# An edge loop of a graph network: fewer chunks by one-hot products, with source and target rows taken the same way

## The chip, the core and the metric

The kernel runs on one core of one Trainium2 chip. TensorE (PE) multiplies matrices into PSUM, VectorE (DVE) and ScalarE (ACT) do elementwise work, GpSimd (POOL) here issues the indirect transfers, and SyncE (SP) issues plain ones. Each engine works through its own queue in order and waits on semaphores. The metric is the device time of one execution in microseconds. The kernel before took 853.11 us, the median of three runs (850.22 to 855.66).

## The reference, cut to what matters

The whole network has four graph layers and four feed-forward layers on 384 nodes of 512 features. The change touches the first graph layer only, and of it only the scores of the 6144 edges. It has 8 heads (H0), and each head works on 128 numbers (2 x HD0) of a row of 1024 (EW):

```python
p = x @ Ww[:512]                 # source part, one row of 1024 for each node
q = x @ Ww[512:] + bw            # target part
s = p[src] + q[dst]              # one row for each edge
score[edge, head] = sum(leaky_relu(s[head's 128 columns], 0.01) * Wa) + ba
```

The kernel writes leaky_relu as 0.01 of the number itself plus 0.99 of its positive part. The first part is linear, so it is worked out once for each node: 8 numbers for a source (`plin`) and 8 for a target, which are columns 1024 to 1031 of the target's row (EL is 1032). Only the positive part has to be worked out for each edge.

## The kernel before, in words

**Set-up.** x is normalized and turned (`xT`). Four weight tiles give first q, then p, in three tiles of 128 nodes and two halves of 512 columns each (`project`, f32). A q tile gets its bias on DVE (L394), its linear part by `linear` (L360, L362), and is stored to `qd` in DRAM from SP. A p tile is copied from PSUM by ACT and stored to `pd`. It is also kept in SBUF as three bf16 parts (`split`): the number rounded to bf16, the rest rounded to bf16, and what then is left (ACT L408 and L412, DVE L411 and L413). The sum of the three parts holds the f32 number nearly whole.

**Edge loop.** The edges go in 48 chunks (EC) of 128, one edge for each partition. There are two ways to a chunk's rows. A *transfer chunk* fetches p's rows into `gp` and q's rows into `gq` by indirect DMAs from POOL (L430, L436), FETCH = 7 chunks ahead, adds them on DVE (L507), and takes the positive part times 0.99 Wa (L509). A *product chunk* fetches only `gq`. Its source rows come from PE: the one-hot matrix `os` of the chunk's sources is turned by three transposes (L384), copied to SBUF by ACT (`osT`, L386), and multiplied with the three tiles and three parts of p (nine bf16 products for each half, L461). The target rows are added in the same PSUM sum by one f32 product with the identity (L463), and DVE reads the sum from PSUM (L516). `by_products` sends 21 chunks this way and 27 by transfers.

For every chunk DVE makes the one-hots `os` and `od` (L371, L372) and copies the target's 8 linear numbers to `lin8` (L503). PE counts edges into `pc` by three products of `os` and `od` (L465). ACT sums seven of the eight heads (L520, an activation and a read of its accumulator for each), and DVE sums the eighth and adds the linear part (L476, L477). POOL then scatters the 8 numbers of each edge into a table in DRAM (`mats`, L446), LAG = 2 chunks later.

**Order.** In one turn c of the loop the code issues: fetches for chunk c+7, scatter of c-2, one-hots of c+3, their turning for c+2, products of c+1, and then chunk c's own work on DVE and ACT. The `issue_after` blocks hold the groups in this order, but between them instructions may be moved, so ACT's copies of turned one-hots stand somewhere between the sums of two chunks. Buffers also hold the order: three PSUM banks `mm` for the sums of products, two `tp` for transposes, five `gp`, eight `gq`, and six `w8` for the 8 numbers, which come free when their scatter has landed. After the loop the table is read back, and the rest of the network follows.

Of the kernel before, what the change touches and what calls it, by code (L numbers as in the profile page):

```python
# [8 lines left out]
F32 = mybir.dt.float32  # L9
F16 = mybir.dt.float16  # L10
BF16 = mybir.dt.bfloat16
# [25 lines left out]
AHEAD = 4  # L37
GQ_BUFS = 8
FETCH = 7
LAG = 2  # L40
# [53 lines left out]
def gnn_ffn_kernel(ctx: ExitStack, tc: tile.TileContext, a, out: bass.AP):  # L94
# [225 lines left out]
    with ExitStack() as s1:  # L320
# [37 lines left out]
        def linear(dst, sb):  # L358
            lin = spare_n[:, 0:2, :].rearrange("p a d -> p (a d)")
            V.tensor_mul(lin.rearrange("p (h k) -> p h k", h=H0),  # L360
                         sb[:, :EW].rearrange("p (h k) -> p h k", h=H0), bc(wa_lin, heads, 1))
            return V.tensor_reduce(dst, lin.rearrange("p (h k) -> p h k", h=H0), AX.X, OP.add)  # L362
# [4 lines left out]
        def hots(c):  # L367

            os_ = ep.tile([P, N], BF16, name="os")
            od = ep.tile([P, N], BF16, name="od")  # L370
            V.tensor_scalar(os_, nodes16, srcf[:, c:c + 1], None, op0=OP.is_equal)  # L371
            V.tensor_scalar(od, nodes16, dstf[:, c:c + 1], None, op0=OP.is_equal)  # L372
            hot[c] = os_, od

        def by_products(c):
            return c < 4 or c % 5 in (1, 3)

        osTs = {}

        def hots_turned(c):  # L380
            if by_products(c):
                pT = pt.tile([P, NT, P], BF16, name="tp")
                for t in range(NT):
                    T.transpose(pT[:, t, :], hot[c][0][:, t * P:(t + 1) * P], identb)  # L384
                osTs[c] = ep.tile([P, NT, P], BF16, name="osT", bufs=2)
                S.copy(osTs[c], pT)  # L386

        ww = stream.take(4, ahead=False)
        for t in range(NT):
            sb = ep.tile([P, EL], F32, name="gq", bufs=GQ_BUFS)  # L390
            for cs in halves:
                p = ps.tile([P, D], F32, name="mm")
                shown = project(p, xT, t, lambda k: ww[k // 2][:, k % 2, cs])
                V.tensor_add(sb[:, cs], p, bw[:, cs])  # L394
            linear(sb[:, EW:], sb)
            ended = V.tensor_scalar(sb[:, EW:], sb[:, EW:], ba, None, op0=OP.add)
            nc.sync.dma_start(qd[t * P:(t + 1) * P, :], sb)

        split, srcs = [], []
        for t in range(NT):  # L400
            with tc.issue_after(shown.ins), tc.issue_after(ended.ins):
                sb = ep.tile([P, EW], F32, name="gp", bufs=5)
                pp = slot()[:, :3 * D].bitcast(BF16).rearrange(
                    "p (i n) -> p i n", i=3)
                for h, cs in enumerate(halves):
                    p = ps.tile([P, D], F32, name="mm")
                    shown = project(p, xT, t, lambda k: ww[2 + k // 2][:, k % 2, cs])
                    S.copy(pp[:, 0, cs], p)  # L408
                    S.copy(sb[:, cs], p)
                    rest = spare_t.rearrange("p k n -> p (k n)")[:, h * D:(h + 1) * D]  # L410
                    V.tensor_sub(rest, sb[:, cs], pp[:, 0, cs])  # L411
                    S.copy(pp[:, 1, cs], rest)  # L412
                    ended = V.tensor_sub(pp[:, 2, cs], rest, pp[:, 1, cs])  # L413
                nc.sync.dma_start(pd[t * P:(t + 1) * P, :], sb)
# [8 lines left out]
        with tc.tile_pool(name="pa", bufs=1, space=bass.MemoryType.PSUM) as pa:  # L423
# [9 lines left out]

            def fetch_target(c):
                gq = ep.tile([P, EL], F32, name="gq", bufs=GQ_BUFS)
                G.indirect_dma_start(out=gq, out_offset=None, in_=qd,  # L436
                                     in_offset=bass.IndirectOffsetOnAxis(ap=dsti[:, c:c + 1], axis=0))
                return gq
# [11 lines left out]
            def multiplied(c):  # L450
# [4 lines left out]
                if by_products(c):  # L455
                    gq, osT = fetched[c][1], osTs.pop(c)
                    z = [ps.tile([P, D], F32, name="mm") for h in range(2)]
                    for h, cs in enumerate(halves):
                        for t in range(NT):
                            for i in range(3):  # L460
                                T.matmul(z[h], lhsT=osT[:, t, :], rhs=split[t][:, i, cs], start=t == 0 and i == 0,  # L461
                                         stop=False)
                        T.matmul(z[h], lhsT=ident, rhs=gq[:, cs], start=False, stop=True)  # L463
                for t in range(NT):
# [13 lines left out]

            multi = {0: multiplied(0)}
            with tc.issue_after(ended.ins):  # L480
                ended = linear(plin[:, 2, :], srcs[2])
            marks = [ended]
            for c in range(EC):
# [7 lines left out]
                if c >= LAG:  # L491
                    marks.append(scatter(c - LAG))
                if c + 3 < EC:
                    hots(c + 3)
                if c + 2 < EC:
                    hots_turned(c + 2)
                if c + 1 < EC:
# [4 lines left out]
                lin = ep.tile([P, H0], F32, name="lin8")  # L502
                V.tensor_copy(lin, gq[:, EW:])  # L503
                w8 = sums[c] = ep.tile([P, H0], F32, name="w8", bufs=6)
# [1243 lines left out]
```

## Time and profile before

| | |
|---|---|
| median of three runs | 853.11 us |
| profiled execution | 855.45 us |
| its span, first to last instruction | 853.5 us |
| mean granted clock of PE | 0.93 |
| PE, DVE, ACT, POOL busy | 87%, 54%, 32%, 27% of the span |
| set-up: first projection to last split of p | 9.9 to 57.0 us |
| chunks 0 to 3, all by products | 53.6 to 79.6 us |
| chunks 4 to 47 | 79.6 to 231.3 us |
| last scatter issued | 234.9 us |

Shares over the whole span say little of the loop, since the rest of the network is a different program. The profile is therefore read by windows: the busy time of each engine between two moments. A timeline row gives start, duration, engine, line, operation, what is written and read, and in brackets how long the engine had been idle and what ended that. Rows of one engine may overlap[...]. What one instruction costs in a row of equal ones is the difference of their starts.

### The profile page before, as it was taken

The page shows a single profiled execution, that of the slowest core. Times are in us where ns is not written, and L with a number is a line of the kernel's source. Part 1 is how long each engine was busy: PE and PEld are TensorE (multiplying, and loading weights), DVE is VectorE, ACT ScalarE, POOL GpSimd, SP SyncE. Part 2 cuts the span into 40 slices and gives each one's busy share as a digit, 9 for nine tenths or more (in the row PEclk, how much of TensorE's full clock was granted, in tenths as well). Part 3 has the DMA queues.
Part 4 walks back from the last instruction along what each step waited for, and adds up shares of the span by engine and source line. Part 5 has one row for each costly group of instructions (what it writes and reads, how often), then busy time and mean ns, then how long its engine had stood idle before and what let it go on. Part 6 is the DMA issues. An engine that isn't in the chain of part 4 may idle for free.

```text
span 853.5 us, 9894 instructions
## 1 busy us (share of the span) xinstructions
PE 746.5 (87%) x2865; PEld 350.2 (41%) x2865; DVE 462.1 (54%) x1199; ACT 273.1 (32%) x1042; POOL 234.5 (27%) x230
## 2 busy tenths in 40 slices
PE   5999888898946769948789999799999999999975
PEld 3444433343434535423355544454444344333432
DVE  4575988887779665376522254745434242421227
ACT  1144766666638723333131111221111111011100
POOL 0046777777600210000100000023333233322122
PEclk9999999899968678985989999889999999999998
DMA  9987877877388011210531463298999999999982
GB/s 336 410 312 243 284 273 258 285 216 238 106 330 311 1 37 53 96 50 12 226 138 49 154 215 108 90 390 320 408 408 403 400 387 396 385 389 391 379 338 104
DMA packets 71197, 211.84 MB, mean 248 GB/s; under 512 B 11615, under 2 KB 16351, under 8 KB 70368
## 3 DMA queue, kind: packets, MB, share of 16 engines
q1 hardware_dynamic: 40592, 135.56, 41.7%
q0 software_dynamic: 19728, 57.97, 19.8%
q10 hardware_dynamic: 10816, 17.61, 5.9%
q8 instruction: 25, 0.41, 0.2%
q14 instruction: 36, 0.29, 0.1%
HBM read 188.46 MB, written 29.83 MB: 256 GB/s over the span
## 4 chain that ended last, share of the span: by engine, by line
PE 56%; DVE 20%; DMA 14%; ACT 6%; issue 3%; DVEq 0%; POOL 0%; SPq 0%; ACTq 0%; POOLq 0%
PE mm L88 14%; DMA w<-in_L_ffn_w_dram 11%; PE acc L88 9%; PE mm L290 8%; PE mm L461 6%; PE mm L1080 4%; PE acc L1093 3%; PE tp L88 3%; PE mm L463 2%; PE mm L952 2%; DVE gp L507 2%; PE acc L965 2%; ACT junk L520 2%; DVE gp L509 2%; DVE mx L88 2%
## 5 line engine op out<-in xcount | busy, mean ns | idle before, releaser
L88 PE MATMUL mm<-w,xe 128*64 128x512 f32 (+1 forms) x504 | 146.1, 598 | 4.9 <-DMA w<-in_L_ffn_w_dram 4.9
L461 PE MATMUL mm<-w,osT 128*128 128x512 bf16 x378 | 92.2, 391 | 9.9 <-ACT osT L386 9.8
L88 POOL DMA_INDIRECT xg<-xnd,src x38 | 39.3, 1034 | 164.9 <-DVE ye L88 140.8
L88 ACT ACTIVATE hide<-mm 128x256 f32<-128x256 f32 x38 | 14.6, 385 | 214.1 <-PE mm L88 214.1
L88 POOL DMA_INDIRECT parts<-ye,dst x35 | 37.9, 1083 | 154.9 <-DVE ye L88 154.9
L88 PEld LDWEIGHTS mm<-w,xe 128*64 128x64 f32 (+1 forms) x504 | 48.2, 148 | 75.0 <-issue 69.1
L88 PE MATMUL acc<-w,hT 128*64 128x512 f32 (+1 forms) x244 | 77.4, 610 | 0.0
L88 DVE TENSOR_TENSOR hide<-hide,mm 128x256 f32<-128x256 f32 x38 | 16.1, 424 | 109.0 <-ACT hide L88 109.0
L290 PE MATMUL mm<-w,xT 128*128 128x512 f32 x144 | 68.6, 633 | 1.8 <-DMA w<-in_L_gnn_Ww_dram 1.2
L520 ACT ACTIVATE junk<-gp 128x128 f32<-128x128 f32 x186 | 54.8, 296 | 39.8 <-issue 22.9
L436 POOL DMA_INDIRECT gq<-qd,dsti x48 | 50.6, 1054 | 59.8 <-DMA qd<-gq 41.8
L461 PEld LDWEIGHTS <-osT 128*128 128x128 bf16 x378 | 36.7, 100 | 65.8 <-issue 17.1
L446 POOL DMA_INDIRECT mat<-w,kidx x48 | 57.0, 1187 | 22.5 <-DMA mat<-w,kidx 4.4
L88 DVE TENSOR_SCALAR ye<-acc,wts 128x512 f32<-128x512 f32 x35 | 26.3, 750 | 59.4 <-PE acc L88 59.4
L520 ACT ACTIVATE junk<-relu 128x128 f32<-128x128 f32 x147 | 43.4, 297 | 18.3 <-DVE relu L516 10.6
L290 PEld LDWEIGHTS mm<-w,xT 128*128 128x128 f32 x144 | 28.8, 204 | 37.7 <-issue 34.4
L516 DVE SCALAR_TENSOR_TENSOR relu<-mm,wa_relu 128x512 f32<-128x512 f32 x42 | 28.1, 684 | 29.3 <-PE mm L463 29.3
L463 PE MATMUL mm<-gq,ident 128*128 128x512 f32 x84 | 43.2, 596 | 0.0
L88 PEld LDWEIGHTS tp<-ident,xg 128*128 128x128 f32 x164 | 23.6, 202 | 28.5 <-issue 24.5
L465 PE MATMUL pc<-od,os 128*128 128x384 bf16 x144 | 29.3, 330 | 6.3 <-DVE od L372 6.3
L520 ACT ACTIVATION_READ_ACCUMULATOR junk<-gp 128x1 f32 x186 | 34.8, 187 | 0.0
L509 DVE SCALAR_TENSOR_TENSOR gp<-gp,wa_relu 128x1024 f32<-128x1024 f32 x27 | 33.1, 1228 | 0.9
(370 smaller groups left out, 1210.0 us busy)
## 6 DMA issues: line engine op xcount, KB each, us to landing
w<-in_L_ffn_w_dram SPq DMA_DIRECT2D x204, 512.0 KB, 12.0
mat<-y ACTq DMA_DIRECT2D x2, 4608.0 KB, 28.4
m<-mat SPq DMA_DIRECT2D x12, 768.0 KB, 7.1
parts<-xg POOLq DMA_DIRECT2D x1, 6144.0 KB, 19.9
w<-parts SPq DMA_DIRECT2D x6, 1024.0 KB, 11.6
w<-in_L_gnn_Ww_dram SPq DMA_DIRECT2D x4, 1024.0 KB, 10.1
w<-in_L_gnn_W_dram ACTq DMA_DIRECT2D x2, 1024.0 KB, 9.0
qd<-gq SPq DMA_DIRECT2D x3, 516.0 KB, 6.7
```

The costliest lines, as they stand in the source:

```text
L88: self.last = getattr(self.engine, name)(*args, **kwargs)
L290: last = T.matmul(p, lhsT=xT[:, k, t * P:(t + 1) * P], rhs=w(k), start=start and k == 0, stop=stop and k == kc - 1)
L436: G.indirect_dma_start(out=gq, out_offset=None, in_=qd, in_offset=bass.IndirectOffsetOnAxis(ap=dsti[:, c:c + 1], axis=0))
L446: return G.indirect_dma_start(out=mats[c % 2], out_offset=bass.IndirectOffsetOnAxis(ap=kidx[:, c:c + 1], axis=0), in_=sums.pop(c), in_offs ...
L461: T.matmul(z[h], lhsT=osT[:, t, :], rhs=split[t][:, i, cs], start=t == 0 and i == 0, stop=False)
L463: T.matmul(z[h], lhsT=ident, rhs=gq[:, cs], start=False, stop=True)
L465: counts.append(T.matmul(pc[t], lhsT=os_[:, t * P:(t + 1) * P], rhs=od, start=c == 0, stop=c == EC - 1))
L509: done = V.scalar_tensor_tensor(g3, g3, 0.0, wide, op0=OP.max, op1=OP.mult)
L516: done = V.scalar_tensor_tensor(g3[:, c8, :], z[h].rearrange("p (h k) -> p h k", h=HH), 0.0, wide[:, c8, :], op0=OP.max, op1=OP.mult)
L520: summed = S.activation(j, g3[:, h, :], AF.Identity, accum_out=w8[:, h:h + 1])
L1080: T.matmul(p, lhsT=gate[:, k, c], rhs=xT[:, k, :], start=k == 0, stop=k == KC - 1)
L1093: T.matmul(p, lhsT=hid[:, m, t * P:(t + 1) * P], rhs=w2[:, m, :], start=m == 0, stop=m == 1)
```

## The change

Fifteen chunks (chunk 0 and those with c % 7 of 1 or 4) now take both source and target rows by products, and 33 take both by transfers. For this, q is also kept in three bf16 parts: its 1024 columns in two idle activation tiles and one new tile (`split_q`), its 8 linear columns in small tiles (`lin_q`). A product chunk turns both one-hots (`osT`, `odT`), sums nine products with p's parts and nine with q's in each half, and gets the 8 linear numbers by nine products of 8 columns into a third PSUM tile, taken from the two `tp` buffers. The f32 product with the identity and the target fetch of these chunks are gone. FETCH is 6, `gq` has five buffers, one-hots have five buffers and are made for chunk c+4, and turned for c+3. The scratch of `linear` is now a buffer of the `relu` ring.

```diff
-GQ_BUFS = 8
-FETCH = 7
+GQ_BUFS = 5
+FETCH = 6
...
-            lin = spare_n[:, 0:2, :].rearrange("p a d -> p (a d)")
+            lin = ep.tile([P, EW], F32, name="relu", bufs=2)
...
-            os_ = ep.tile([P, N], BF16, name="os")
-            od = ep.tile([P, N], BF16, name="od")
+            os_ = ep.tile([P, N], BF16, name="os", bufs=5)
+            od = ep.tile([P, N], BF16, name="od", bufs=5)
...
         def by_products(c):
-            return c < 4 or c % 5 in (1, 3)
+            return c == 0 or c % 7 in (1, 4)
...
             if by_products(c):
-                pT = pt.tile([P, NT, P], BF16, name="tp")
-                for t in range(NT):
-                    T.transpose(pT[:, t, :], hot[c][0][:, t * P:(t + 1) * P], identb)
-                osTs[c] = ep.tile([P, NT, P], BF16, name="osT", bufs=2)
-                S.copy(osTs[c], pT)
+                turned_hots[c] = []
+                for i, name in enumerate(("osT", "odT")):
+                    pT = pt.tile([P, NT, P], BF16, name="tp")
+                    for t in range(NT):
+                        T.transpose(pT[:, t, :], hot[c][i][:, t * P:(t + 1) * P], identb)
+                    turned_hots[c].append(ep.tile([P, NT, P], BF16, name=name, bufs=2))
+                    S.copy(turned_hots[c][i], pT)
+
+        def three(dst, part, c, src, rest):
+            S.copy(dst[:, 0, c], part)
+            V.tensor_sub(rest, src, dst[:, 0, c])
+            S.copy(dst[:, 1, c], rest)
+            return V.tensor_sub(dst[:, 2, c], rest, dst[:, 1, c])
...
+        kept = [slot() for t in range(NT)]
+        kept_q = [v.rearrange("p k n -> p (k n)") for v in (spare_t, spare_n)] + [one.tile([P, 3 * D], F32, name="qq")]
...
             nc.sync.dma_start(qd[t * P:(t + 1) * P, :], sb)
+            qq = bf16s(kept_q[t])
+            for h, cs in enumerate(halves):
+                three(qq, sb[:, cs], cs, sb[:, cs], kept[t][:, 3 * D:])
+            ql = one.tile([P, 3, H0], BF16, name=f"ql{t}")
+            ended = three(ql, sb[:, EW:], slice(0, H0), sb[:, EW:], one.tile([P, H0], F32, name="qrest"))
+            split_q.append(qq)
+            lin_q.append(ql)
...
             def fetch_target(c):
+                if by_products(c):
+                    return None
...
                     z = [ps.tile([P, D], F32, name="mm") for h in range(2)]
+                    z.append(pt.tile([P, H0], F32, name="tp"))
+                    parts_ = [(i, t) for i in range(3) for t in range(NT)]
                     for h, cs in enumerate(halves):
-                        for t in range(NT):
-                            for i in range(3):
-                                T.matmul(z[h], lhsT=osT[:, t, :], rhs=split[t][:, i, cs], start=t == 0 and i == 0,
-                                         stop=False)
-                        T.matmul(z[h], lhsT=ident, rhs=gq[:, cs], start=False, stop=True)
+                        for n, (w, whole) in enumerate(((osT, split), (odT, split_q))):
+                            for i, t in parts_:
+                                T.matmul(z[h], lhsT=w[:, t, :], rhs=whole[t][:, i, cs],
+                                         start=n == 0 and (i, t) == (0, 0), stop=n == 1 and (i, t) == (2, NT - 1))
+                    for i, t in parts_:
+                        T.matmul(z[2], lhsT=odT[:, t, :], rhs=lin_q[t][:, i, :], start=(i, t) == (0, 0),
+                                 stop=(i, t) == (2, NT - 1))
...
+            hots_turned(2)
+            hots(3)
...
+                if c + 4 < EC:
+                    hots(c + 4)
                 if c + 3 < EC:
-                    hots(c + 3)
-                if c + 2 < EC:
-                    hots_turned(c + 2)
+                    hots_turned(c + 3)
...
-                V.tensor_copy(lin, gq[:, EW:])
+                V.tensor_copy(lin, gq[:, EW:] if z is None else z[2])
```

More of the change, by code (lines that the diff above doesn't have):

```diff
@@ L375, in by_products @@
         def by_products(c):
-            return c < 4 or c % 5 in (1, 3)
-        osTs = {}
+            return c == 0 or c % 7 in (1, 4)
+        turned_hots = {}
         def hots_turned(c):
             if by_products(c):
-                pT = pt.tile([P, NT, P], BF16, name="tp")
-                for t in range(NT):
-                    T.transpose(pT[:, t, :], hot[c][0][:, t * P:(t + 1) * P], identb)
-                osTs[c] = ep.tile([P, NT, P], BF16, name="osT", bufs=2)
-                S.copy(osTs[c], pT)
+                turned_hots[c] = []
[10 more added lines that the diff above has]
+            return V.tensor_sub(dst[:, 2, c], rest, dst[:, 1, c])
         ww = stream.take(4, ahead=False)
+        kept = [slot() for t in range(NT)]
+        kept_q = [v.rearrange("p k n -> p (k n)") for v in (spare_t, spare_n)] + [one.tile([P, 3 * D], F32, name="qq")]
+        bf16s = lambda w: w[:, :3 * D].bitcast(BF16).rearrange("p (i n) -> p i n", i=3)
+        split_q, lin_q = [], []
         for t in range(NT):
@@ L395, in gnn_ffn_kernel @@
             linear(sb[:, EW:], sb)
-            ended = V.tensor_scalar(sb[:, EW:], sb[:, EW:], ba, None, op0=OP.add)
+            V.tensor_scalar(sb[:, EW:], sb[:, EW:], ba, None, op0=OP.add)
             nc.sync.dma_start(qd[t * P:(t + 1) * P, :], sb)
+            qq = bf16s(kept_q[t])
[5 more added lines that the diff above has]
+            lin_q.append(ql)
         split, srcs = [], []
@@ L402, in gnn_ffn_kernel @@
                 sb = ep.tile([P, EW], F32, name="gp", bufs=5)
-                pp = slot()[:, :3 * D].bitcast(BF16).rearrange(
-                    "p (i n) -> p i n", i=3)
+                pp = bf16s(kept[t])
                 for h, cs in enumerate(halves):
@@ L407, in gnn_ffn_kernel @@
                     shown = project(p, xT, t, lambda k: ww[2 + k // 2][:, k % 2, cs])
-                    S.copy(pp[:, 0, cs], p)
                     S.copy(sb[:, cs], p)
[L410 to L413, printed above, removed]
+                    ended = three(pp, p, cs, sb[:, cs], kept[t][:, 3 * D:])
                 nc.sync.dma_start(pd[t * P:(t + 1) * P, :], sb)
@@ L455, in multiplied @@
                 if by_products(c):
-                    gq, osT = fetched[c][1], osTs.pop(c)
+                    osT, odT = turned_hots.pop(c)
                     z = [ps.tile([P, D], F32, name="mm") for h in range(2)]
+                    z.append(pt.tile([P, H0], F32, name="tp"))
+                    parts_ = [(i, t) for i in range(3) for t in range(NT)]
                     for h, cs in enumerate(halves):
-                        for t in range(NT):
-                            for i in range(3):
-                                T.matmul(z[h], lhsT=osT[:, t, :], rhs=split[t][:, i, cs], start=t == 0 and i == 0,
-                                         stop=False)
-                        T.matmul(z[h], lhsT=ident, rhs=gq[:, cs], start=False, stop=True)
+                        for n, (w, whole) in enumerate(((osT, split), (odT, split_q))):
[5 more added lines that the diff above has]
+                                 stop=(i, t) == (2, NT - 1))
                 for t in range(NT):
```

## The prediction

> **What bounds the kernel now.** The profile's second part shows the edge loop as the stretch where POOL reads 7 (slices 4 to 11, 64 to 235 us). Only this loop and the set-up before it are changed, so I read the windows of the loop, then its waits, then the chain of waits. Columns of the first fence: PE, PEld, DVE, ACT and POOL busy us (instructions), granted clock, DMA share, GB/s.
>
> ```profile
> 79.60:231.30 151.70, 133.02 (x563) 60.69 (x562) 126.28 (x303) 100.53 (x631) 114.45 (x102) 0.97 0.73 236
> ```
> ```profile
> DVE relu L516 <- PE mm L463: 18.5, 13, 2.6
> ...
> ACT junk L520 <- DMA mat<-w,kidx: 12.9, 6, 4.4
> ...
> PE mm L461 <- ACT osT L386: 9.8, 9, 3.0
> ```
>
> At 79.6 us DVE starts chunk 4; at 231.3 it is done with chunk 47. No engine is full; three are close. POOL looks 75% busy, but its timeline shows 0.30 us of nothing ahead of every instruction, so 102 instructions cost 114.45 + 102 x 0.30 = 145.1 of 151.7 us, 1.42 us each. DVE's only real idle time is 18.5 us before the relu of a product chunk, waiting for PE. PE in turn waits for ACT's copy of the turned one-hots, and ACT now and then for a scatter that POOL sent late (its w8 ring has six buffers). The chain of waits repeats one turn per five chunks:
>
> ```profile
> 95.84 1.14 DVE gp L507
> 97.01 1.22 DVE gp L509
> 99.43 1.02 DVE gp L507
> 100.75 1.23 issue
> 101.99 2.15 ACT junk L520 x14
> 104.56 2.12 PE mm L461 x9
> 106.68 0.86 PE mm L463 x2
> 107.53 1.94 PE mm L461 x9
> 109.48 0.87 PE mm L463 x2
> 110.37 0.69 DVE relu L516
> ```
>
> Two transfer chunks on DVE, ACT's sums, then a product chunk's 5.8 us on PE in the open. From relu to relu (94.15 to 110.37) 16.2 us pass for five chunks; DVE's own work for them is 14.8 (below). The rest is the second of two product chunks that stand only two apart: its products can't start before ACT has copied the turned one-hots, which stand in ACT's queue behind the sums of two chunks.
>
> **Prices.** DVE, from its timeline: start to start a transfer chunk takes 3.39 to 3.68 us (82.46 to 86.05; 88.26 to 91.65), I take 3.45; a product chunk without a wait 2.21 to 2.32 (86.05 to 88.26), I take 2.25. PE:
>
> ```profile
> 59.67 0.33 PE L384 MATMUL tp<-identb,os 128*128 128x128 bf16 x3
> 59.84 2.11 PE L461 MATMUL mm<-w,osT 128*128 128x512 bf16 x9
> 61.78 1.02 PE L463 MATMUL mm<-gq,ident 128*128 128x512 f32 x2
> 62.64 2.10 PE L461 MATMUL mm<-w,osT 128*128 128x512 bf16 x9
> ```
>
> Start to start: nine bf16 products 1.94 us (216 ns each), one f32 product (two records) 0.86, three transposes 0.17 (55 ns each), and three counts `pc` 0.49.
>
> **The change in the loop, by engine.**
> PE: a product chunk had 18 x 0.216 + 2 x 0.86 = 5.6 us; now 36 x 0.216 = 7.8, plus nine products of 8 columns and three more transposes. No 8-column product is in the trace; each has weights of its own, as the transposes do, so I take their 55 ns: 0.5 us a chunk. The ends are 25 ns, the issue floor in the Trainium skill ("TensorE: Matmul & The Clock Gate", Back-to-back issue gap), and 81 ns, which the same section gives for pairs of weight load and 128-column matmul. That rule speaks against swapping one f32 product for strings of small ones: 15 x 9 + 45 more transposes make 180 pairs, 14.6 us by the rule, 9.9 by the row; I take the row, as this kernel's pairs ran at it. With two sets of transposes (0.33) a product chunk is 8.6 us. All chunks: 21 x 5.8 + 48 x 0.49 = 145 before, 15 x 8.6 + 23.5 = 153 after.
> DVE: six chunks go from 2.25 to 3.45: +7.2 us. The 8-wide copy from PSUM instead of from `gq` is below 0.1 either way.
> POOL: 15 target gathers go, 6 source gathers come: 123 instructions become 114, -9 x 1.42 = -12.8 us.
> ACT: 30 copies of turned one-hots instead of 21, +9 x 0.46 = 4.1 us; ACT has 51 us free in the window, and only the copies' place in the queue counts.
> DMA: 9 gathers of about 0.5 MB less, at a share of 0.73; nothing waits on a gather (L507 has no idle time before it), so nothing for that.
> Fewer buffers: with FETCH 6 and five `gp` and `gq` buffers, the gather for chunk c+6 takes the buffer of chunk c-1, so POOL can't begin turn c before DVE's reduce of c-1 is done; behind that gather on POOL stand the target gather and the scatter of c-2. The gather lands 5.8 us after issue (median of the DMA view) and is wanted six chunks, 19 us, later: no cost while POOL lags DVE by less than 13 us. `linear`'s scratch in the relu ring and q's parts in idle activation tiles move no instruction.
>
> **What decides is the order.** Product chunks now lie 3 and 4 apart, and one-hots and their turning are issued one chunk earlier. In the changed queues ACT's copies for the next product chunk stand within or just before the sums of the last one. New is a ring: z[2] and both turned one-hots share the two `tp` buffers, so the target transposes of the next product chunk wait for DVE's `lin` copy of the last; behind them on PE stand the counts and the next z, on which DVE waits.
> Gap of three, from `lin` to `lin`: DVE needs 2 transfer chunks and its own relus, 3 x 1.0 + 2 x 2.4 + 1.3 = 9.1 us. PE: transposes, counts and ACT's copy about 1.0, then 7.8 + 0.5, 0.2 to hand over: 9.5. Stall 0.4 us. Gap of four: DVE 12.5, PE 3.2 (behind seven sums, 2.05, and two copies) + 8.3 = 11.5: none. So seven chunks take about 22.0 us, 3.14 a chunk, where five took 16.2, or 3.25.
> POOL: seven chunks hold 10 gathers and 7 scatters, 17 x 1.42 = 24.1 us, more than 22.0, as before 13 x 1.42 = 18.5 against 16.2. POOL falls behind up to the w8 ring, then holds ACT, and catches up in the last chunks, which have no gathers left.
>
> **The set-up.** Its head on DVE grows: 12 subtractions at 0.61 us start to start and 6 of 8 columns, 8 us, and DVE's queue has them after the last q tile, ahead of p's splits. ACT gets 12 copies at 0.5. The p evacuations on ACT stand behind q's, but PSUM has three buffers and the first must be free at 43 us; it is at about 42. DVE from 36.1: 8 for q's splits, some 0.5 of waits on ACT, then p's 12 subtractions (7.3), three `linear` (7.3, the last behind the splits), four pairs of one-hots (1.8). The last split lands at about 59 instead of 57; PE's last projection waits for the one-hots of chunk 1 queued ahead of it and ends at 55 instead of 53.5. Then only two product chunks come, not four: z of chunk 0 ends at 63, of chunk 1 at 72 (7.8 + 0.5 + 0.5 each), and DVE starts chunk 2 at about 73.5; with 1 us for hand-overs, 74.5. The source gathers wait for the store of p (62.2 now, about 63.5 then) and the first is there by 70. So 46 chunks remain at 74.5, where 44 remained at 79.6: minus 5.1 us, but two chunks more.
>
> **The sum.** By the chain: 74.5 + 46 x 3.14 = 219; by POOL: 104 instructions remain when scatter 0 goes out at 74, 74 + 104 x 1.42 = 222 for the last scatter, which comes 4.5 us after DVE's end (235.9 against 231.3 now). Both ask for 218 to 219. The same sums for the kernel as it is give 79.6 + 44 x 3.25 = 223, and it took 231.3: 8 us went to two late scatters (4.4 and 4.1 us) and the cold clock after them. I keep half of that, since POOL still falls behind: 219 + 4 to 5 = 223.5, 7.6 us less. The profiled execution took 855.45 (span 853.5 and 1.95 around it); it would take 847.9. It lies above the median, and 853.11 - 7.6 gives **845.5**.
>
> Cold clock: after more than 2.5 us without work PE ran at half speed:
>
> ```profile
> 166.84 4.05 PE L461 MATMUL mm<-w,osT 128*128 128x512 bf16 x9
> ...
> 171.87 2.11 PE L461 MATMUL mm<-w,osT 128*128 128x512 bf16 x9
> ```
>
> This cost 1.9 us here (idle 2.5 us before) and 1.7 at 202.08 (idle 3.0). The skill's page named above (Part 1) wants an idle window of some 3.4 us; the row has it after less, and I go by the row. Changed, PE works 20.6 of 22 us, so by either no such gap should come up and up to 3.6 us come back (half taken); if gaps do, a z of 36 products starts with a run at half speed.
>
> **Rivals.**
> 1. *Full cover* (15%): with 9 POOL instructions less, no scatter is late; the loop ends at 219, total 841. For it: POOL's balance is 6% better by chunk. Against: 24.1 is still above 22.0.
> 2. *No gain* (10%): product chunks keep the stall of now, 18.5 / 17 = 1.1 us; 13 x 1.1 = 14 us on DVE's own 74.5 + 33 x 3.45 + 13 x 2.25 = 217.6 gives 232: 854. For it: PE's z is longer by 2.7 us. Against: copies are issued one chunk earlier.
> 3. *PE becomes the bound* (20%, slower): the `tp` ring chains DVE's `lin`, PE's transposes, ACT's copy and z in series. If ACT's copy falls behind the seven sums (2.05 us) and PE waits until its clock halves (1.9), each of the seven gap-of-three chunks costs 4 us: +28, total 873. From 1.1 us at each of them the gain is gone, from 2.3 on it is slower by over 1%. For it: z is 8.3 us against 9.1 of cover; any slip shows. Against: the changed order of ACT.
>
> **Numbers.** My own case (55%) reaches from 840 to 850, a little under half beyond 1% (8.5 us, what a measurement here can tell from no change). Faster 0.25 + 0.15 = 0.40; same 0.30 + 0.10 = 0.40; slower 0.20. The unknown prices (8-column products, 11 us between their ends on PE, two thirds hidden; set-up 3 us; POOL 1.42 to 1.50, 8 us) make 836 to 850 and rival 2 and the near part of 3 take it up to 858.
>
> **What would show it.** Right: DVE adds chunk 2 at 72 to 76 us; idle before the relus under 8 us in all; last scatter at 225 to 230; granted clock in the loop 0.97 or more. Wrong: PE idle on ACT's odT for over 2 us per product chunk, the last split later than 62 us, or gathers late at L507's successor.

## The result and the profile after

The changed kernel takes 855.92 us (median of 20 runs, 852.38 to 861.54); the kernel before, run beside it, 852.09 us (20 runs). The ratio is **1.0053, with a 95% interval of 1.0034 to 1.0072**: some 4.5 us slower, where 7.6 us faster was forecast. The profiled execution took 856.2 us, its span 854.1. The rest of the network is not what made it slower: from the first maximum on the table `m` to the end of the span, 609.8 us pass before and 605.8 after (602.0 to 609.8 in the 20 profiles of this document). The loss lies ahead of that point, which came at 243.69 us and now comes at 248.24. In this profile it lies behind the loop: DVE's last sum ends at 230.6 us (231.2 before), and from there to the maximum 17.7 us pass instead of 12.5. So two things need a cause: why the loop gained 0.6 us and not 7.6, and why its tail grew.

First the window of the loop in the profile after, with the columns of the prediction's first fence.

```profile
79.60:231.30 151.70, 134.57 (x775) 65.08 (x773) 133.84 (x305) 105.46 (x653) 116.07 (x99) 0.99 0.71 223
```

The clock is now 0.99 (0.97 before). PE does a little more, and DVE 7.6 us more, near the 7.2 that were forecast. The line to stop at is POOL's: three instructions less than before in the same time, and 1.6 us more busy. Then the waits in the same window, as total, number and longest in us:

```profile
ACT junk L543 <- DMA mat<-w,kidx: 18.5, 11, 4.4
...
DVE gp L530 <- DMA gp<-pd,srci: 5.7, 5, 2.1
...
DVE relu L539 <- PE mm L480: 2.8, 4, 1.3
```

DVE's wait for products fell from 18.5 us to 2.8, as forecast. Two others grew: ScalarE waits longer for landed scatters (12.9 us before), and DVE now waits for gathered rows, which it never did before. Both come from POOL. Its groups from 73 to 240 us (instructions, busy us, mean ns, idle before), first before, then after:

```profile
L446 POOL DMA_INDIRECT mat<-w,kidx x47 | 56.0, 1191 | 22.2 <-DMA mat<-w,kidx 4.4 <-DVE lin L503 3.6 <-issue 3.3
L436 POOL DMA_INDIRECT gq<-qd,dsti x38 | 40.5, 1066 | 15.3 <-issue 6.7 <-PE mm L463 4.0 <-DVE od L372 1.2
L430 POOL DMA_INDIRECT gp<-pd,srci x22 | 22.9, 1041 | 7.0 <-ACT junk L520 4.3 <-issue 1.5 <-DVE w L476 0.6
```
```profile
L463 POOL DMA_INDIRECT mat<-w,kidx x48 | 53.5, 1115 | 32.9 <-issue 17.8 <-DVE w L498 8.8 <-DVE lin L526 2.7
L453 POOL DMA_INDIRECT gq<-qd,dsti x28 | 37.1, 1325 | 8.8 <-DVE od L372 3.4 <-issue 3.4 <-DVE gp L532 0.6
L445 POOL DMA_INDIRECT gp<-pd,srci x28 | 33.2, 1186 | 8.5 <-ACT junk L543 5.5 <-issue 1.8 <-DMA mat<-w,kidx 0.9
```

Before, 107 instructions take 119.4 us, 1.12 each. After, 104 take 123.8 us, 1.19 each: a target gather costs 0.26 us more than it did. The timeline shows where from (start, duration):

```profile
132.43 1.21 DVE L530 TENSOR_TENSOR gp<-gp,gq 128x1024 f32<-128x1024 f32 x1
132.46 2.02 POOL L453 DMA_INDIRECT gq<-qd,dsti  x1 [0.30 <-DVE od L372]
```

A gather whose issue usually takes 0.94 to 0.99 us takes 2.02 when it begins just after DVE's add of `gp` and `gq` has begun. Which of the two begins first is what counts:

```profile
151.03 0.99 POOL L463 DMA_INDIRECT mat<-w,kidx  x1 [0.30 <-DVE w L497]
151.72 1.22 DVE L530 TENSOR_TENSOR gp<-gp,gq 128x1024 f32<-128x1024 f32 x1
152.33 1.45 POOL L445 DMA_INDIRECT gp<-pd,srci  x1 [0.30 <-ACT junk L543]
```

In this profile 40 issues overlap an add from 73 to 240 us. The 28 that began 0.02 to 1.06 us after it all ended 0.81 to 0.87 us after the add did, wherever inside it they began. The 12 that began before it, or together with it, took at most 1.05 us.

Below, **hold-up** is the sum, over POOL's instructions from 40 to 242 us that take more than 1.1 us, of their time above 0.96. It was 16.1 us in 23 instructions before and is 25.7 us in 33 after; 19.3 us of that lie under the add (each issue is put to the operation that it overlaps longest), nearly all the rest under DVE's other operations with two f32 operands in SBUF (3.0 us under the multiply with `wa_relu`, 2.5 under the product in `linear` in the set-up), none under the relu that reads PSUM.

The chain of waits shows what it does. Three turns of the loop go through a gather issued too late, and the end through late scatters (start, duration):

```profile
137.32 8.78 DMA gp<-pd,srci
...
163.86 8.64 DMA gp<-pd,srci
...
187.73 5.29 DMA gp<-pd,srci
```
```profile
230.39 5.09 DMA mat<-w,kidx
...
235.55 3.08 issue
...
238.84 2.63 DMA mat<-w,kidx
```

### The profile page after: what moved, and what is told of

It reads as the page before. It is cut to its first block, busy times and chain, and to the rows that moved or that the text cites. A ratio compares the mean times of both kernels' runs of the same rounds, so it can differ in the third digit from the quotient of the medians.

```text
span 854.1 us, 10391 instructions
## 1 busy us (share of the span) xinstructions
PE 745.2 (87%) x3105; PEld 354.9 (42%) x3105; DVE 478.5 (56%) x1217; ACT 282.6 (33%) x1069; POOL 235.5 (28%) x221
## 4 chain that ended last, share of the span: by engine, by line
PE 44%; DMA 27%; DVE 20%; ACT 5%; issue 3%; POOL 1%; SPq 0%; DVEq 0%; ACTq 0%; POOLq 0%
DMA w<-in_L_ffn_w_dram 20%; PE mm L88 8%; PE acc L88 7%; PE mm L480 7%; PE mm L290 6%; PE mm L1103 4%; PE acc L1116 3%; DMA gp<-pd,srci 3%; PE mm L975 2%; DVE gp L530 2%; DVE gp L532 2%; PE acc L988 2%; PE tp L88 2%; DMA m<-mat 2%; DMA mat<-w,kidx 1%
## 5 line engine op out<-in xcount | busy, mean ns | idle before, releaser
L543 ACT ACTIVATE junk<-gp 128x128 f32<-128x128 f32 x228 | 67.2, 296 | 37.3 <-issue 13.7
L88 DVE TENSOR_TENSOR hide<-hide,mm 128x256 f32<-128x256 f32 x38 | 16.1, 424 | 108.9 <-ACT hide L88 108.9
L480 PE MATMUL mm<-w,osT 128*128 128x512 bf16 x270 | 65.0, 387 | 7.7 <-ACT osT L388 7.7
L453 POOL DMA_INDIRECT gq<-qd,dsti x33 | 43.7, 1324 | 50.2 <-DMA qd<-gq 40.1
L445 POOL DMA_INDIRECT gp<-pd,srci x33 | 39.0, 1182 | 18.3 <-DMA pd<-gp 8.5
L530 DVE TENSOR_TENSOR gp<-gp,gq 128x1024 f32<-128x1024 f32 x33 | 40.2, 1219 | 5.7 <-DMA gp<-pd,srci 5.7
L480 PEld LDWEIGHTS <-osT 128*128 128x128 bf16 x270 | 26.1, 99 | 41.7 <-ACT osT L388 11.0
L543 ACT ACTIVATION_READ_ACCUMULATOR junk<-gp 128x1 f32 x228 | 42.6, 187 | 0.0
L532 DVE SCALAR_TENSOR_TENSOR gp<-gp,wa_relu 128x1024 f32<-128x1024 f32 x33 | 40.5, 1226 | 1.1
L480 PEld LDWEIGHTS <-odT 128*128 128x128 bf16 x270 | 26.4, 98 | 32.1 <-ACT junk L543 0.3
L543 ACT ACTIVATE junk<-relu 128x128 f32<-128x128 f32 x105 | 31.0, 296 | 20.8 <-DMA mat<-w,kidx 10.1
## 6 DMA issues: line engine op xcount, KB each, us to landing
mat<-y ACTq DMA_DIRECT2D x2, 4608.0 KB, 27.4
```

Source lines behind the costliest of these rows:

```text
L88: self.last = getattr(self.engine, name)(*args, **kwargs)
L445: G.indirect_dma_start(out=gp, out_offset=None, in_=pd, in_offset=bass.IndirectOffsetOnAxis(ap=srci[:, c:c + 1], axis=0))
L453: G.indirect_dma_start(out=gq, out_offset=None, in_=qd, in_offset=bass.IndirectOffsetOnAxis(ap=dsti[:, c:c + 1], axis=0))
L480: T.matmul(z[h], lhsT=w[:, t, :], rhs=whole[t][:, i, cs], start=n == 0 and (i, t) == (0, 0), stop=n == 1 and (i, t) == (2, NT - 1))
L530: V.tensor_add(gp, gp, gq[:, :EW])
L532: done = V.scalar_tensor_tensor(g3, g3, 0.0, wide, op0=OP.max, op1=OP.mult)
```

## The experiments

Theory A: POOL sets the pace of the loop, and DVE's operations with two f32 operands in SBUF hold its transfers up; six more transfer chunks bring more of them. Rivals: B, the chain of products, copies and DVE sets the pace; C, only the tail is slower; D, the smaller rings are. Ratios are to the kernel before in the same group of runs. That kernel took 869.6 and 869.9 us in groups 1 and 5, and 851 to 852 us elsewhere, so these two groups are read within themselves only. Where these 18 us come from is not known: groups 1, 2 and 3 carry the same chip number on record.

| kernel | ratio, 95% interval | hold-up us (instructions) | start of DVE's last sum, us | first `m`, us |
|---|---|---|---|---|
| before | 1 | 16.1 (23) | 231.0 | 243.7 |
| after | 1.0053 (1.0034 to 1.0072) | 25.7 (33) | 230.4 | 248.2 |
| *group 1:* after again | 1.0008 (0.9985 to 1.0030) | 27.4 (32) | 247.5 | 259.3 |
| after, zero row in PSUM | 1.0512 (1.0479 to 1.0545) | 2.7 (4) | 291.4 | 303.5 |
| before, zero row in PSUM | 1.0392 (1.0362 to 1.0423) | 0.6 (2) | 273.9 | 290.3 |
| after, half the scatters | 0.9765 (0.9733 to 0.9796) | 27.4 (31) | 229.1 | 241.6 |
| *group 2:* after, add as reduction | 1.0004 (0.9985 to 1.0022) | 25.5 (31) | 228.1 | 245.7 |
| before, add as reduction | 0.9994 (0.9976 to 1.0012) | 15.4 (22) | 231.4 | 243.4 |
| after, summing gathers | 1.0280 (1.0250 to 1.0310) | 31.3 (47) | 253.2 | 269.9 |
| after, add in halves | 1.0061 (1.0036 to 1.0085) | 29.2 (56) | 231.5 | 249.0 |
| *group 3:* **after, no pairs** | **0.9878 (0.9858 to 0.9899)** | **2.7 (4)** | **218.8** | **230.9** |
| **before, no pairs** | **0.9933 (0.9914 to 0.9951)** | **0.6 (2)** | **225.1** | **236.4** |
| after, rows early | 1.0044 (1.0019 to 1.0069) | 25.0 (31) | 233.1 | 247.5 |
| before, order alone | 1.0035 (1.0016 to 1.0053) | 19.7 (27) | 231.8 | 246.5 |
| *group 4:* after, 12 w8 | 1.0093 (1.0064 to 1.0122) | 25.0 (32) | 228.9 | 246.6 |
| before, order and 12 w8 | 1.0022 (1.0001 to 1.0042) | 21.2 (29) | 229.5 | 247.3 |
| after, order undone | 1.0273 (1.0242 to 1.0305) | 28.7 (29) | 253.1 | 265.1 |
| **after, 17 by products** | **0.9969 (0.9950 to 0.9988)** | 20.5 (24) | 225.2 | 238.1 |
| *group 5:* after, 18 by products | 1.0052 (1.0026 to 1.0077) | 21.5 (25) | 254.7 | 267.7 |
| 17 by products, no pairs | 0.9991 (0.9972 to 1.0010) | 2.6 (4) | 247.5 | 261.0 |

The hold-up is counted to 242 us in every row, so loops that end later are not counted whole. To the last scatter it is 28.2 us (33) for the changed kernel again, 32.3 (49) with summing gathers, 30.3 (31) with the order undone and 23.1 (27) with 18 chunks by products.

### Once more, and half the scatters

The first kernel is the changed one unedited. The other leaves scatters out:

```diff
-                    marks.append(scatter(c - LAG))
+                    if c % 2:
+                        sums.pop(c - LAG)
+                    else:
+                        marks.append(scatter(c - LAG))
```

> The changed kernel unchanged, to see which of its late places come back. Theory A (GpSimd paces the loop, and each DVE add of two f32 tiles in SBUF holds up one of its DMA issues): again about 33 GpSimd issues between 40 and 242 us that take longer than 1.1 us, some 25 us above 0.96 in all, DVE's loop end near 230.5 us, time within 0.3% of 855.9 us. Theory C (only the tail differs: the 3.08 us without any visible reason before the last scatter at 238.84 us): if that gap is gone here, the profiled span must be about 3 us shorter; if it comes back, it belongs to the kernel.

> Leaves out every second scatter of the loop (those of odd chunks but the last), 23 GpSimd issues less; the rest is the changed kernel. Theory A: GpSimd no longer falls behind, gathers and the w8 ring are never late, DVE's loop ends at 217 to 222 us and the total is 843 to 848. Theory B: no change of the loop end beyond 2 us. Theory D (the narrower buffers of gathered rows, five instead of eight, cost the time by themselves): gathers stay late at DVE's add (L530 waits over 4 us) although GpSimd has room.

The hold-up came back (27.4 us in 32), so it belongs to the kernel. The 3 us gap ahead of the last scatter did not come back, and neither did the loss: from the end of DVE's last sum to the first `m` 11.6 us pass, and the ratio is 1.0008, not to be told from 1. The expectation that the time would stay within 0.3% of 855.9 us failed, since all of group 1 is slow. With 23 scatters less DVE's last sum comes 18.4 us earlier than in the unedited kernel of the same group. That fits a loop paced by POOL and speaks against B. It is no clean proof: it also takes 23 transfers away, and this group has a trouble of its own. The granted clock in the window of the loop is 0.92 instead of 0.99, and PE stops inside its strings of products without a visible wait: its products stand still for 6.4 us in 8 places (none in the first profile of the changed kernel), and its weight loads show the same (1.9 us on this row in the first profile, 0.3 at the longest):

```profile
PEld L480 <- issue: 16.3, 36, 2.5
```

### One operand out of SBUF: two attempts that settled nothing on time

In both kernels a zero row and `wa_relu` were put into spare columns of the PSUM banks of the counts, and the add became `gp` plus the zero row:

```diff
+            wide_p = bank[0][:, N:]
...
+            zero_p = bank[1][:, N:]
...
-                    V.tensor_add(gp, gp, gq[:, :EW])
+                    V.tensor_add(g3, g3, bc(zero_p, [P, H0, 2 * HD0], 1))
```

> Leaves out the target term of the 33 transfer chunks: gp is added to a zero row in PSUM instead of to gq, and the relu factor is read from PSUM too, so none of DVE's ops on 1024 columns in a transfer chunk reads two operands from SBUF; all gathers, scatters and products stay. Theory A: the GpSimd issues above 1.1 us fall from 33 to under 10 and their excess from 25.7 to under 6 us, DVE's loop ends at 219 to 224 us instead of 230.5 (its own work then sets the end), total 845 to 850. Theory B (the chain of products, copies and DVE sets the pace) : loop end within 2 us of 230.5 and total within 2 us of the changed kernel's.

> The same edit in the kernel before: the target term of its 27 transfer chunks left out, zero row and relu factor in PSUM. Theory A: it has 23 long issues with 16.1 us excess to lose, so it gains 3 to 7 us, less than the changed kernel does, and against it the changed kernel with the same edit is 2 to 6 us faster, in the direction that was forecast. Theory B: no gain, and the order of the two kernels stays as it is (changed one 4 us slower).

The hold-up is gone from the loop in both; the 2.7 us left lie in the set-up. But both are far slower. The counts `pc` and DVE now wait for each other over the shared banks, which the kernels without the edit don't do; in the changed kernel, from 72 to 245 us:

```profile
DVE gp L536 <- PE pc L491: 23.8, 4, 6.5
...
PE pc L491 <- DVE gp L536: 13.3, 13, 3.2
```

So the place of the hold-up is seen, its price is not. Next the add alone became an operation with one operand and the same length, a reduction over an axis of length 1 (1.2 us on DVE, as the add):

```diff
-                    V.tensor_add(gp, gp, gq[:, :EW])
+                    V.tensor_reduce(gp, gp.rearrange("p (n o) -> p n o", o=1), AX.X, OP.add)
```

> Leaves out the target term of the 33 transfer chunks in the changed kernel: DVE's add of gp and gq (two f32 operands in SBUF) becomes a reduction over an axis of length 1 (one operand, the same 1024 columns, about the same 1.1 to 1.2 us on DVE), with no other wait added. Theory A: none of GpSimd's long issues lies under it any more; the excess falls from 26 to 4 to 10 us (what the multiply by wa_relu, with two operands in SBUF too, still holds up), and the first add of the m tables (248.2 and 259.3 us in the two profiles so far) comes 6 to 14 us earlier against the changed kernel on the same chip; ratio to the kernel before 0.985 to 0.993. Theory B: within 2 us of the changed kernel.

> The same edit in the kernel before (27 adds). Theory A: excess falls from 16 to under 7 us; gain of 3 to 8 us, ratio 0.991 to 0.997, and the changed kernel with this edit is faster than this one by 3 to 8 us, as the prediction had it for the change. Theory B: no gain, and the changed kernel with the edit is not faster than this one.

The expectation failed in an instructive way. Nothing is held up under the add any more, but 25.5 us remain: 25 instructions and 21.9 us now lie under the multiply by `wa_relu`, which had held up 8 for 3.0 us. The issues now fall on whichever such operation is left, so removing one of two leaves the hold-up as it was. The kernel before with the edit shows the same (15.4 of 16.1 us left) and no gain. The changed kernel's ratio fell from 1.0053 to 1.0004, though, with DVE's last sum 2.3 us earlier. The edit also takes `gq` from the add's operands, so its buffer comes free some 1.2 us earlier; whether that is the gain is not shown.

### Both operations with one operand

```diff
-                    V.tensor_add(gp, gp, gq[:, :EW])
...
-                    done = V.scalar_tensor_tensor(g3, g3, 0.0, wide, op0=OP.max, op1=OP.mult)
+                    V.tensor_reduce(gp, gp.rearrange("p (n o) -> p n o", o=1), AX.X, OP.add)
...
+                    done = V.tensor_reduce(gp, gp.rearrange("p (n o) -> p n o", o=1), AX.X, OP.max)
```

> Leaves out the target term and the relu of the 33 transfer chunks in the changed kernel: both the add of gp and gq and the multiply by wa_relu become reductions over an axis of length 1 (one operand from SBUF, 1024 columns, about 1.2 us each), so DVE's queue keeps its length and no op of it on transfer chunks reads two operands from SBUF. The edit of the add alone only moved the long GpSimd issues from the add to the multiply (23 us excess there). Theory A (GpSimd is held up by two-operand DVE ops, and that sets the loop): excess falls from 25 to under 5 us, no gather and no w8 buffer is late, DVE's loop ends at 218 to 223 us, the first add of m comes 6 to 12 us before the changed kernel's 248.2; ratio to the kernel before 0.986 to 0.994. Theory A' (GpSimd is held up, but what sets the loop is DVE's own work and the landing of scatters): excess falls as much and the loop ends within 3 us of 228 to 230.

> The same edit in the kernel before. Theory A: excess falls from 16 to under 3 us, the loop gains 3 to 6 us, and the changed kernel with the edit is 3 to 7 us faster than this one. Theory A': no gain here either, and the two stay within 2 us.

This decides it for A in what the loop could have gained. DVE's queue keeps its length (1.21 and 1.22 us for the two reductions), POOL's number of instructions too; from 73 to 240 us the changed kernel's POOL groups read

```profile
L463 POOL DMA_INDIRECT mat<-w,kidx x48 | 47.6, 992 | 36.3 <-DVE w L498 11.6 <-DVE w L497 6.7 <-DVE lin L526 4.5
L453 POOL DMA_INDIRECT gq<-qd,dsti x28 | 27.0, 965 | 8.5 <-issue 4.0 <-DVE gp L532 0.9 <-DVE gp L530 0.9
L445 POOL DMA_INDIRECT gp<-pd,srci x28 | 26.6, 949 | 10.3 <-ACT junk L543 7.0 <-issue 2.1 <-DVE w L497 0.3
```

and an issue right beside such a reduction takes its usual time:

```profile
127.52 0.94 POOL L445 DMA_INDIRECT gp<-pd,srci  x1 [0.30 <-ACT junk L543]
127.64 1.21 DVE L530 TENSOR_REDUCE gp<-gp 128x1024 f32<-128x1024 f32 x1
128.76 0.99 POOL L463 DMA_INDIRECT mat<-w,kidx  x1 [0.31 <-issue]
```

The waits of DVE for gathers and of ScalarE for landed scatters are gone from the list. The changed kernel's DVE ends at 219.0 instead of 230.6 us. In time, the edit is worth 1.75% to the changed kernel (1.0053 to 0.9878), some 15 us, and 0.67% to the kernel before, some 5.5 us. The add's reduction alone, which frees `gq` early too but keeps the hold-up, was worth 0.5% and nothing, so at least 1.26% and some 0.6% are the price of the hold-ups. **Without them the order of the two kernels turns round**: 840.87 against 846.26 us, 5.4 us faster. That it is near the 7.6 that were forecast is in part luck, since the forecast set the changed kernel against one that keeps its hold-ups.

### Shorter adds, and adds left to the transfers

```diff
-                    V.tensor_add(gp, gp, gq[:, :EW])
+                    for h in range(2):
+                        V.tensor_add(gp[:, halves[h]], gp[:, halves[h]], gq[:, halves[h]])
```

> The changed kernel with each add of gp and gq issued as two of 512 columns. Theory A: a held-up issue waits for half an add only; excess per long issue falls from 0.9 to about 0.5 us, total from 26 to about 15 to 20 us, against some 2 to 4 us more work on DVE; ratio to the changed kernel 0.992 to 1.0. Theory B: 2 to 4 us slower than the changed kernel.

Excess for each held-up instruction falls from 0.8 to 0.5 us, as expected, but 56 are held up instead of 33. The expected 15 to 20 us in all became 29.2, and there is no gain (1.0061). The second kernel gathers q's rows first and lets the source gather add p's rows to them, two chunks later (with rings of seven rows, and fetches seven chunks ahead):

```diff
+                    G.indirect_dma_start(out=fetched[c][:, :EW], out_offset=None, in_=pd, compute_op=OP.add,
                                          in_offset=bass.IndirectOffsetOnAxis(ap=srci[:, c:c + 1], axis=0))
...
-                    V.tensor_add(gp, gp, gq[:, :EW])
```

> The changed kernel with DVE's add taken out by letting the source gather add its rows onto the gathered target rows (an accumulating transfer issued two chunks after the plain one); same number of GpSimd issues, ring of seven rows. DVE loses 33 x 1.22 = 40 us. Theory A: no add is left to hold GpSimd up, so the loop ends 8 to 16 us earlier, at the pace of GpSimd (114 x 1.27 us) or PE; ratio 0.98 to 0.99. If the accumulating transfer takes GpSimd or the DMA engines much longer than the plain one (1.0 us, 5.8 us to landing), DVE waits on gathers instead and the kernel is slower than before. Theory B: no gain beyond what DVE's shorter chain brings.

The second of the three expectations came true. An adding gather costs POOL 1.64 us on average (so the hold-up in the table counts these too), and DVE waits 16.4 us for rows, ScalarE 50.1 us for landed scatters:

```profile
L444 POOL DMA_INDIRECT gq<-pd,srci x28 | 46.0, 1641 | 29.9 <-DMA gq<-qd,dsti 13.8 <-DMA mat<-w,kidx 11.4 <-issue 4.6
```

### The tail

```diff
+                if c == 36:
+                    with tc.issue_after(summed.ins):
+                        gamma, beta = row("L0_gnn_gamma"), row("L0_gnn_beta")
...
-        with tc.issue_after(summed.ins):
-            gamma, beta = row("L0_gnn_gamma"), row("L0_gnn_beta")
```

> The changed kernel with the two broadcast rows gamma and beta loaded in chunk 36 instead of at the end of the loop, so that they don't move (512 KB, some 4 us) while the last scatters land. Theory C (the tail costs what was forecast to be gained): the last scatters land in 2.2 to 2.7 us instead of 4 to 5, the last one is issued 4 to 5 us after DVE's last sum instead of 8.5, the first add of m comes 2 to 5 us earlier, ratio to the kernel before 0.999 to 1.003. If the late scatter is GpSimd's own (some 2 us without a visible reason between its last two issues), it gains under 1.5 us.

No gain (1.0044). The last scatter is issued 5.4 us after DVE's last sum instead of 8.2, but that sum comes later. Its chain has the same silent gap ahead of the last scatter as the changed kernel's:

```profile
235.02 0.28 POOL mat L463
235.30 3.08 issue
...
238.60 2.13 DMA mat<-w,kidx
```

What POOL does in these 3.08 us the profile doesn't show; it stays open. In the changed kernel POOL has no backlog there: it stands idle for 6.2 us ahead of the last scatter. The long tail goes with the hold-ups where POOL paces the loop: with no pairs, from DVE's last sum to the first `m` takes 11.9 us, as in the kernel before (12.5), not 17.7. But in the slow group 1 the hold-ups came with a short tail, so what makes the tail long is not shown.

### The order of the one-hots

The kernel before with one-hots and their turning one chunk earlier, and the changed kernel with them back at the old place (five buffers kept). The diff is that of the kernel before:

```diff
-        wa_relu = one.tile([P, 2 * HD0], F32, name="wa_relu")
+        wa_relu = wa
...
-            os_ = ep.tile([P, N], BF16, name="os")
-            od = ep.tile([P, N], BF16, name="od")
+            os_ = ep.tile([P, N], BF16, name="os", bufs=5)
+            od = ep.tile([P, N], BF16, name="od", bufs=5)
...
+            hots_turned(2)
+            hots(3)
...
-                if c + 3 < EC:
-                    hots(c + 3)
-                if c + 2 < EC:
-                    hots_turned(c + 2)
+                if c + 4 < EC:
+                    hots(c + 4)
+                if c + 3 < EC:
+                    hots_turned(c + 3)
```

> The kernel before with one part of the change alone: one-hots and their turning one chunk earlier (five buffers of each), sources by products and targets by transfers as before. If the wait of DVE's relu on products (18.5 to 24 us) came from the order and was worth its length, that wait falls under 10 us and the loop ends 4 to 8 us earlier, ratio 0.990 to 0.996. If GpSimd and the landing of scatters pace the loop (A), DVE meets late gathers instead and the ratio is 0.997 to 1.003.

> The changed kernel with the order part undone: one-hots three chunks ahead and turned ones two ahead, as before. If the order was what decides, DVE's relu waits grow from 6 us to 15 us or more and the time by 5 us or more (ratio to the kernel before over 1.010). Theory A: relu waits grow, the waits for late gathers and landed scatters shrink, ratio within 0.003 of the changed kernel's 1.005.

In the kernel before the relus now wait 7.6 us in all from 72 to 245 us, instead of 24.3, and nothing is gained: ScalarE waits longer for scatters that land too late (12.9 us before), and the hold-up rises from 16.1 to 19.7 us, with the same 27 transfer chunks.

```profile
ACT junk L522 <- DMA mat<-w,kidx: 34.1, 16, 4.9
```

In the changed kernel the order is worth 2.2%, which A had not expected. Undone, PE's granted clock in the window of the loop falls to 0.88, and the relus wait 32.8 us instead of 6.0:

```profile
DVE relu L537 <- PE mm L480: 32.8, 18, 3.6
```

So the order brings nothing when it is added and costs much when it is taken out. That fits two engines near their limits, where whichever is later sets the pace.

### The rings

```diff
-                w8 = sums[c] = ep.tile([P, H0], F32, name="w8", bufs=6)
+                w8 = sums[c] = ep.tile([P, H0], F32, name="w8", bufs=12)
```

> The changed kernel with 12 instead of 6 buffers of the sums w8 that the scatters read, so that ScalarE no longer waits for landed scatters (18.5 us in 11 waits). Theory D (small rings cost the time): that wait is gone and the loop ends 4 us or more earlier, ratio to the kernel before 0.996 to 1.001. Theory A (GpSimd, held up by two-operand DVE ops, sets the pace): the wait is gone, but DVE's waits for late gathers or the lateness of the last scatters grow by as much, excess stays at 23 to 28 us, ratio 1.002 to 1.008 as for the changed kernel.

> The kernel before with the earlier one-hots alone and 12 buffers of w8 (with 6 ScalarE waited 34.1 us for landed scatters). Theory D: that wait is gone and the order's gain comes through, loop end 4 us or more earlier, ratio 0.990 to 0.996. Theory A: GpSimd (138.8 us busy over 123 issues) only falls further behind and the scatters or gathers are late by as much; ratio 1.000 to 1.005.

The waits for landed scatters are gone in both, and neither gains (1.0093 and 1.0022): DVE waits 8.2 us for gathers in the first (5.7 with 6 buffers), and in the second 5.2 us for gathers and 17.0 for products. D falls for the w8 ring. The rings of gathered rows were not tried larger.

### Fewer instructions on POOL

```diff
-            return c == 0 or c % 7 in (1, 4)
+            return c == 0 or c % 3 == 1
```

> The changed kernel with 17 chunks by products (chunk 0 and every third) and 31 by transfers: four GpSimd issues and two pairs of two-operand DVE ops less, two products more (PE some 151 us from 72 us on). Theory A: 4 x 1.26 us and two hold-ups of about 0.8 us less for GpSimd, so the last scatter 4 to 7 us earlier if PE keeps up, ratio 0.997 to 1.001. Theory B (PE and its copies pace the loop): two products of 8.6 us more, less DVE's cover; loop end 4 to 10 us later, ratio 1.010 to 1.017.

**This one lies below both kernels**, by a little: 847.87 us, ratio 0.9969 to the kernel before. DVE's waits for gathers are gone, hold-up is 20.5 us, the relus wait 14.5 us for products, and PE, at a granted clock of 1.00, is now busy 149.9 of 151.7 us:

```profile
79.60:231.30 151.70, 149.86 (x879) 74.64 (x892) 130.27 (x312) 107.91 (x660) 110.47 (x97) 1.00 0.67 213
```

One more chunk by products (the diff is against the kernel of 17), and 17 with no pairs (the two edits of that experiment, on the kernel of 17):

```diff
-            return c == 0 or c % 3 == 1
+            return c == 0 or c % 14 in (1, 4, 7, 9, 12)
```

> The changed kernel with 18 chunks by products, 30 by transfers (two GpSimd issues less than with 17). With 17 chunks DVE waited 14.5 us for products in 15 relus, so PE is close to setting the pace. GpSimd still the limit (A): another 2 to 4 us less, ratio to the kernel before 0.992 to 0.996. PE the limit (B, from 17 on): one product of 8.6 us more on PE, partly under DVE's transfers, two places only two chunks apart; 2 to 8 us slower than with 17, ratio 0.999 to 1.006.

> The split of 17 and 31 with the target term and relu of the transfer chunks left out (reductions with one operand in place of the add and the multiply). If GpSimd's hold-ups still set that kernel's loop: excess from 20 to under 4 us and another 5 us or more gained (ratio under 0.991). If with 17 products PE sets it: excess falls as much, the relu waits for products stay at 12 to 20 us, ratio within 0.003 of 0.9969.

These ran in the other group in which PE stops in its strings (8.9 and 14.4 us of such stops on L480's weight loads), so 1.0052 and 0.9991 can't be set beside 0.9969. Within the group, 17 with no pairs lost its hold-ups (2.6 us), its relus still wait 15.7 us for products, and it can't be told from the kernel before; whether 18 by products or the hold-ups limit the kernel of 17 in the faster groups stays open.

## Why the prediction was wrong

- **Set-up: right.** Last split at 59.2 us (about 59), last projection ends at 55 (55), z of chunks 0 and 1 done at 63 and 71.6 (63 and 72), chunk 2's add at 73.30 (73.5 to 74.5).
- **PE, DVE and the order: right.** Relu waits 6.0 us from 70 to 240 us (under 8), clock 0.99 (0.97 or more); DVE's own 33 x 3.45 + 13 x 2.25 = 143.1 us from 73.3 gives 216.4, and 12.0 us of waits fill most of the rest to 230.6. Nine 8-column products take 0.23 us, not 0.5. (The 11 us between their two ends don't come out either: 135 x 56 ns are 7.6.)
- **The failing step is POOL's line: "123 instructions become 114, -9 x 1.42 = -12.8 us".** Busy time from 40 to 242 us went from 135.1 to 136.1 us. The count was right; 1.42 was not a price that stays. It was 0.97 us of work, 0.30 between instructions, and 0.15 of hold-up, for which the text has no term. Nine instructions at 1.27 are 11.4 us less; hold-up grew by 9.6, so 1.8 us were left. The number of transfer chunks explains a part of that only: 33 instead of 27 would make 19.7 us of 16.1. It is 25.7, since 2.1 us came in the set-up and the issues of the loop fell on adds more often and for longer. The order alone, with 27 chunks, raised it to 19.7. What places the issues there stays open.
- **The range for POOL's price did not save it.** "POOL 1.42 to 1.50, 8 us" holds what came: (136.1 + 114 x 0.30) / 114 = 1.49. By the prediction's own sum that asks for the last scatter at 74 + 104 x 1.49 = 229; it ended at 240.3. Idle time ahead of that scatter makes 5.9 us of the difference, and POOL's other waits are not split here.
- **"I keep half of that, since POOL still falls behind: 219 + 4 to 5"** failed with it. With the hold-ups taken away the loop did end at 219.0 us and the kernel took 840.9 (the first rival's 219 and 841). With them it ended at 230.6. The wrong sign that the text named, late gathers, is what is seen.
- **The tail** was put at 4.5 us from DVE's end to the end of the last scatter's issue; it took 9.7. That it is slower, and not only no faster, lies here, and its cause is open.
- **The rivals.** The third (PE the bound through order and half clock, 873 us) named a real danger: with the order undone the kernel takes 872.5. That the two numbers agree may be luck, since that edit is not the slip the rival describes. It wasn't what made this kernel slower: the relus wait 6.0 us. No case on the slower side had POOL falling further behind in it.

## What to carry to other kernels

Don't multiply a mean duration by a change in number before looking at its spread: list the long instructions of the group and what the other engines do in those moments, and which of the two began first. Here a transfer whose issue began inside one of DVE's two-operand f32 operations in SBUF waited for its end, so moving rows from products to transfers brought POOL new issues and new hold-ups. And when two engines are both near the limit, take a wait away on one only after asking how late the other is.

## What the runs showed of the hardware

- An indirect DMA that takes POOL 0.94 to 0.99 us takes up to 2.07 when its issue begins while DVE is in an add or multiply of 1024 f32 columns with both operands in SBUF; in the changed kernel it ended 0.8 to 0.9 us after that operation. One that had begun before the operation took at most 1.08 us (26 cases in the kernels before and after). There is no such hold-up with an operand in PSUM, nor under a reduction of the same length. The Trainium skill ("SBUF — State Buffer", Who interferes with whom) says that a DVE instruction with two SBUF inputs contends with a GpSimd instruction that reads SBUF; the runs agree, if an indirect DMA, which takes its row numbers from SBUF, counts as one. The same section infers that such an add does not hold up the writing of a DMA's descriptors. The runs don't say which part of the issue waits, but the row with 2.02 us shows that the issue as a whole does.
- The hold-up did not shrink with the number of such operations: with one of two removed 25.5 of 25.7 us remained, with the adds cut in half 29.2.
- An adding gather costs POOL 1.64 us on average where the plain one beside it costs 1.06.
- The same kernel takes 852 us in some groups of runs and 870 in others, and in the two profiles of the changed kernel the difference, 11 us, lies ahead of the first `m`, with a granted clock of 0.92 against 0.99 in the window of the loop.
